# Spectrum split by parity, pixels in four quadrants of the array, the blurred part on 66 columns

## The chip, the cores and the metric

The kernel runs on one core of one Trainium2 chip. The metric is the device time of one execution in microseconds (us). Five engines matter: PE is TensorE (PEld is its weight load), ACT is ScalarE, DVE is VectorE, POOL is GpSimd, and SP is the queue from which nearly all DMAs are issued.

## The reference

The input is x, 16 images of 64 channels of 128 x 128 pixels, float32. Two layers follow each other.

```python
# layer 0: Hartley transform, 20x20 low modes mixed over channels, transformed back,
# blurred (9-tap Gauss) over all four axes, then masked along the last axis
x_ht = dht_2d(x)
out_ht[:, :, :20, :20] = compl_mul2d(x_ht[:, :, :20, :20], w1)
y = gaussian_smoothing_4d(dht_2d(out_ht) / (H * W)) * (abs(fftfreq(W)) <= 0.25)
# layer 1
h = group_norm(y)
h = irfft2(block MLP on the first 32 x 32 modes of rfft2(h)) + h     # _afno
h = h + y                                                            # residual
f = gelu(conv1x1(group_norm(h)))                                     # features
out = mean over 2 shared of gelu(conv1x1(f)) + sum over the top 4 of 16 experts of
      gate * gelu(conv1x1(f)) + h                                    # gate from the mean of f
```

`abs(fftfreq(W)) <= 0.25` holds for 65 of the 128 columns: the first 33 and the last 32.

## The kernel before

**Stages.** A *forward* stage streams x from HBM and takes the 20 x 20 Hartley modes of each image, blurred over the images, into `x2`. A *mixing* stage multiplies them with the weights (`wk`), 40 matmuls for each of 11 values of `k1`, copies the result out of PSUM into two tiles `om` (lines 298 to 303, ACT and DVE in turn), and blurs over channels. A *spectrum* stage (lines 376 to 570) takes group statistics, the 32 x 32 modes that layer 1 needs (line 548, with the 3.2 MB table `spec`) and the first half of the block MLP, and leaves per image `o1d` (MLP activations) and `od`, `ond` (the 20 x 20 modes of layer 0) in HBM. Then comes the *image* stage, which takes three quarters of the time and which most of the change is about.

**One image** in the image stage goes through these pieces:

- `spectrum`: one DMA brings `o1d[b]` into `s`, eight DMAs bring modes of layer 0 into columns 64 to 104 of the tile `bm` (the one buffer of that name, partitions x 32 x 105).
- `spectrum_f` (2 calls): 64 matmuls each for the second half of the MLP; ACT copies the PSUM tile into columns 0 to 63 of `bm` (line 629).
- `rows` (8 calls): inverse transform along the rows, for 4 channels of each half. Its matmuls (line 647) already use 64 x 64 quadrants of the array; ACT copies to `u` (line 652).
- `pixels` (8 calls): inverse transform along the columns, for 16 pixel rows. A matmul (line 669) contracts 107 rows of `u` (64 of layer 1's spectrum, 41 of layer 0's modes, 2 for the bias `b2`) with the table `inv2`, on 128 output partitions (two pixel rows x 64 channels). ACT adds a bias into `h` (line 677); DVE takes statistics of `h` (line 681).
- `norm2` (3 steps), `feature` (8 calls, lines 732 and 736), `gate` (8 steps), and 48 `group`s: a group is one expert or shared layer on a 128 x 1024 piece. PE (line 826), ACT's Gelu into `g` (line 831), and DVE's multiply-add into `h` (line 834) do one group. After the fourth expert of a piece, two DMAs store it (`store`, line 845).

**Order.** One list of pieces is sorted and emitted; each engine executes its instructions in that order. The list gives each call a place relative to the first of the image's own 48 groups:

```python
PIECES = (
    (lambda box, i: spectrum(box), (-84,)),
    (spectrum_f, (-57, -50)),
    ...
    (rows, (-50, -49, -48, -48, -48, -40, -39, -38)),
    (pixels, (-36, -32, -28, -24, -24, -24, -23, -23)),
    (group, range(NG)),
)
```

A place of -24 is thus after half of the 48 groups of the image before. ACT's part of a piece is emitted one piece later, DVE's part one further (`on_act`, `on_dve`). PSUM tiles named `pe` have three buffers of two banks, shared by all the pieces. `h` has 14 buffers of which an image uses 8; `u` and `bm` have one each. So `rows` of an image come after `pixels` of the one before it, and `spectrum` and `spectrum_f` after its `rows`.

Of the kernel before, what the change touches and what calls it, by code (L numbers as in the profile page):

```python
# [11 lines left out]
F32 = mybir.dt.float32  # L12
AF = mybir.ActivationFunctionType
ALU = mybir.AluOpType
# [4 lines left out]
NB, C, N = 16, 64, 128  # L19
K = 20  # L20
NM = K * K
CH = 100
# [7 lines left out]
HR, KC = 52, 105  # L30
KU = KC + 2
CL = C // 2
# [22 lines left out]
def constant_tables():  # L55
# [22 lines left out]
    a32 = th * np.outer(m32, n)  # L78
    inv1, inv2 = np.zeros((128, 2, N)), np.zeros((KU, N))
    for r in (0, 64):  # L80
# [5 lines left out]

    inv2[KC], inv2[KC + 1] = inv2[:32].sum(0), inv2[32:64].sum(0)
    c, s = np.cos(a32).sum(0), np.sin(a32).sum(0)
    bias = np.array([[c, s], [-s, c]])

    by_half = lambda t: t.reshape(-1, 2, 2, N // 2).transpose(0, 1, 3, 2).reshape(-1, 2 * N)
    inv1, bias = by_half(inv1), by_half(bias)

# [37 lines left out]
    for loc in range(5):  # L131
# [12 lines left out]
        "inv2": inv2,  # L144
        "bias": bias,
        "spec": chunked(spec.reshape(NM, 2 * MD * MD)),
# [13 lines left out]
def hartley_afno_moe_kernel(ctx: ExitStack, tc: tile.TileContext, a: dict, out: bass.AP):  # L160
# [26 lines left out]
    with tc.tile_pool(name="modes", bufs=1) as mp:  # L187
# [6 lines left out]
        with tc.tile_pool(name="f_x", bufs=10) as xp, tc.tile_pool(name="f_t", bufs=2) as tp, \  # L194
# [9 lines left out]
            def along_columns(b, t1):  # L204
# [20 lines left out]
                for bo in range(NB):  # L225
                    g = float(gb[bo, b])
                    if g == 0.0:
                        continue
                    to = x2[:, 0, bo, :]
                    if bo in seen:  # L230
                        nc.vector.scalar_tensor_tensor(to, xf, g, to, ALU.mult, ALU.add)
                    else:
                        nc.vector.tensor_scalar(to, xf, g, None, ALU.mult)
                        seen.add(bo)
                    if not gb[bo, b + 1:].any():
                        nc.scalar.mul(x2[0:C, 1, bo], x2[C:P, 0, bo], -1.0)
                        nc.scalar.copy(x2[C:P, 1, bo], x2[0:C, 0, bo])

# [37 lines left out]
        vec = load(const, "vec", [P, V_N])  # L276
        spec = load(sc, "spec", [CH, 4, 2 * MD * MD])
        exw = load(sc, "exw", [P, C, NE])

        with tc.tile_pool(name="m_o", bufs=1) as op, \  # L280
# [7 lines left out]
            for k1 in range(K // 2 + 1):  # L288
# [8 lines left out]
                lo, up = ps[0:C, :, :, :, 0], ps[C:P, :, :, :, 1]  # L297
                nc.scalar.copy(lok[:, k1], lo[:, :, 0])
                nc.vector.tensor_copy(upk[:, k1], up[:, :, 0])
                if k1 % (K // 2):  # L300
                    nc.scalar.copy(lok[:, K - k1, 0:1], lo[:, 0:1, 1])
                    nc.scalar.copy(lok[:, K - k1, K // 2 - 1:0:-1], lo[:, 1:, 1])
                    nc.vector.tensor_copy(upk[:, K - k1, ::-1], up[:, :, 1])


            for b0 in range(0, NB, 8):
                for cc in range(2):
# [7 lines left out]
                    for h in range(2):  # L315
# [4 lines left out]
                        else:  # L320
                            nc.vector.tensor_copy(dst, src)


    s3 = ctx.enter_context(ExitStack())
# [8 lines left out]

    b2 = kp.tile([2, C], F32, name="b2t")
    for ri in range(2):
        nc.sync.dma_start(b2[ri:ri + 1], a["b2"][32 * ri:32 * ri + 1, 0:C])
    bias = load(kp, "bias", [2, 2, N])
    b2r = kp.tile([P, 2, C], F32, name="b2r")
    b2x = dram.tile([2, N, C], F32, name="b2x")
    inv1 = load(kp, "inv1", [P, 2, N])  # L340
    inv2 = load(kp, "inv2", [KU, N])
    grp = load(kp, "grp", [P, P])
# [18 lines left out]
    nc.vector.memset(ones_e, 1.0)  # L361
    bm = kp.tile([P, CL, KC], F32, name="bm")
    nc.gpsimd.memset(bm, 0.0)
# [7 lines left out]
    with tc.tile_pool(name="s_w", bufs=2) as sw, tc.tile_pool(name="s_o", bufs=1) as so, \  # L371
# [134 lines left out]
        def prepare():  # L506
            for hf in range(2):
# [6 lines left out]
                nc.scalar.copy(v2b[C:P, hf, 1], v2[C:P, 0, cs])  # L514
            ps = pp3.tile([P, 512], F32, name="pso")
            for i in range(2):
                nc.tensor.matmul(ps[:, i * C:(i + 1) * C], lhsT=bias[:, i], rhs=b2, start=True, stop=True)
            nc.scalar.copy(b2r.rearrange("p i c -> p (i c)"), ps[:, 0:2 * C])
            nc.sync.dma_start(b2x.rearrange("i n c -> n i c"), b2r)

# [49 lines left out]
    with s3:  # L570
# [6 lines left out]
        u = up_.tile([P, N, C], F32, name="u")  # L577
        nc.sync.dma_start(u[KC:KU], b2x)

# [17 lines left out]
        def flush():  # L597
            done(0)
            while behind_d:
                behind_d.popleft()()  # L600

        def spectrum(box):

            b = box["b"]
            s = box["s"] = sp.tile([P, MD * MD], F32, name="s")
            nc.sync.dma_start(s, o1d[b].rearrange("r c k -> (r c) k"))
            for h in range(2):
                r, i = (0, 32) if h else (64, 96)
                cs = slice(h * CL, (h + 1) * CL)
                for at, q, src in ((r, 0, od), (i, 1, od), (r + 1, 21, od), (i, 21, ond)):  # L610
                    nc.sync.dma_start(bm[at:at + K, :, 64 + q:64 + q + K], src[b, :, cs, :])

        def spectrum_f(box, q):
# [13 lines left out]
            def evacuate():  # L627
                bmf = bm[:, :, 0:64].rearrange("p c (r j) -> p r c j", r=2)
                nc.scalar.copy(bmf[:, :, :, q * 16:(q + 1) * 16], ps.rearrange("p i r c -> p r c i"))
                if q:  # L630
                    box["spectrum"] = True
# [3 lines left out]
        def rows(box, q):  # L635


            if q == 0:
                if "spectrum" not in box:
                    flush()  # L640
            ps = ps2.tile([P, 2, 4, N], F32, name="pe")
            for i in range(4):
                for part, h in ((0, 0), (1, 0), (0, 1), (1, 1)):
                    k0 = C * (h ^ part)
                    rs = slice(k0, k0 + (HR if part else C))
                    cs = slice(64, KC) if part else slice(0, 64)
                    nc.tensor.matmul(ps[cs, h, i, :], lhsT=bm[rs, 4 * q + i, cs],  # L647
                                     rhs=inv1[rs, part], start=True, stop=True)

            def evacuate():  # L650
                dst = u[0:KC].rearrange("p n (h s) -> p h s n", h=2)[:, :, 4 * q:4 * q + 4, :]
                nc.scalar.copy(dst.rearrange("p h s n -> p n h s"),  # L652
                               ps[0:KC].rearrange("p h s n -> p n h s"))
                box["rows"] = q + 1

            on_act(evacuate)

        def pixels(box, t):
# [7 lines left out]
            ps = ps2.tile([P, 2, 512], F32, name="pe")  # L666
            for r in range(8):
                row = t * 8 + r
                nc.tensor.matmul(  # L669
                    ps[:, r // 4, r % 4 * N:(r % 4 + 1) * N],  # L670
                    lhsT=u[0:KU, 2 * row:2 * row + 2, :].rearrange("p h c -> p (h c)"),
                    rhs=inv2, start=True, stop=True)

# [189 lines left out]
        def step(name, make):  # L863
# [7 lines left out]

        PIECES = (
            (lambda box, i: spectrum(box), (-84,)),
            (spectrum_f, (-57, -50)),
            (feature, (-5, -4, -3, -2, -2, -2, -2, 0)),
            (step("norm", norm2), (-19, -16, -10)),
            (step("gate", gate), (2, 3, 5, 7, 8, 8, 10, 12)),
            (rows, (-50, -49, -48, -48, -48, -40, -39, -38)),
            (pixels, (-36, -32, -28, -24, -24, -24, -23, -23)),
            (group, range(NG)),  # L880
# [79 lines left out]
```

## Time and profile before

| What | us |
|---|---|
| median of 3 runs (lowest, highest) | 1857.68 (1852.98, 1859.34) |
| the profiled execution | 1848.89 |
| its span on the core | 1846.9 |
| forward stage, to the last matmul of line 212 | 0 to 253 |
| mixing, first to last matmul of line 294 | 261 to 289 |
| spectrum stage, to the first spectrum_f | 289 to 474 |
| first Gelu of a group, image 0 to image 15 | 530.1 to 1778.9 |
| end | 1846.9 |

The profile is of one execution. "Busy" is the union of an engine's instructions, and matmul ends are modelled. From the first group of one image to that of the next the trace shows 83.3 to 84.4 us (the last such step, with nothing after it to prepare, 76.5), so 15 steps make 1249 us of the 1847. The table is read with that number in mind: a saving of 1 us per image is 15 us of the whole.

### The profile page before, as it was taken

How to read it: one execution, taken by the hardware profiler on the slowest of the kernel's cores; microseconds unless marked ns; L12 is line 12 of the kernel's file. 1: busy time of each engine (PE TensorE's matmuls, PEld its weight loads, DVE VectorE, ACT ScalarE, POOL GpSimd, SP SyncE). 2: the span in 40 equal slices, each digit the busy share in tenths (PEclk: the TensorE clock that was granted, in tenths of full speed). 3: DMA queues.
4: the chain of work that ended last, by engine and by line, in shares of the span. 5: the costliest groups of instructions: out<-in, count | busy, mean ns of one | idle time of the engine just before them, and what ended most of it. 6: DMA issues, size and time to landing. Idle time of an engine off the chain costs nothing. (4 is left out here: it accounts for less than half of the span.)

```text
span 1846.9 us, 55817 instructions
## 1 busy us (share of the span) xinstructions
PE 1701.5 (92%) x24644; PEld 940.8 (51%) x24644; DVE 1270.7 (69%) x1774; ACT 1378.3 (75%) x1690; POOL 120.9 (7%) x140
## 2 busy tenths in 40 slices
PE   6777769999899999999999999999999999999996
PEld 6776765333645455454545555454545455554521
DVE  1233432322249788797979797797979797887988
ACT  2343343112488998989898999989898999989897
POOL 0000002003010101010110101010100101010110
PEclk8899988999999999999999999999999999999998
DMA  9999841115212222222332222322232322222023
GB/s 337 319 322 326 285 145 48 69 52 145 47 25 70 48 81 57 84 36 82 57 72 58 59 82 36 99 41 81 37 86 53 71 72 46 72 57 71 27 72 92
DMA packets 136129, 181.00 MB, mean 98 GB/s; under 512 B 94201, under 2 KB 95414, under 8 KB 135658
## 3 DMA queue, kind: packets, MB, share of 16 engines
q1 hardware_dynamic: 132192, 171.73, 33.1%
q0 software_dynamic: 3696, 5.71, 1.2%
q8 instruction: 193, 3.16, 0.7%
q14 instruction: 48, 0.39, 0.1%
HBM read 98.29 MB, written 79.11 MB: 96 GB/s over the span
## 5 line engine op out<-in xcount | busy, mean ns | idle before, releaser
L834 DVE SCALAR_TENSOR_TENSOR h<-g,wt,h 128x1024 f32<-128x1024 f32 x512 | 620.9, 1275 | 85.2 <-ACT g L831 85.2
L831 ACT ACTIVATE g<-pe,wl 128x1024 f32<-128x1024 f32 x512 | 539.4, 1131 | 8.9 <-PE pe L826 8.2
L826 PE MATMUL pe<-f,wl 64*64 64x512 f32 x4096 | 494.7, 600 | 1.3 <-issue 0.4
L834 DVE SCALAR_TENSOR_TENSOR h<-g,h 128x1024 f32<-128x1024 f32 x256 | 301.6, 1220 | 56.1 <-ACT g L831 56.1
L831 ACT ACTIVATE g<-pe,vec_sb 128x1024 f32<-128x1024 f32 x256 | 278.7, 1135 | 20.6 <-PE pe L826 20.4
L669 PEld LDWEIGHTS pe<-inv_sb,u 107*128 107x128 f32 x2048 | 234.4, 192 | 64.9 <-ACT g L831 33.2
L826 PEld LDWEIGHTS pe<-f,wl 64*64 64x64 f32 x4096 | 135.6, 132 | 237.3 <-ACT g L831 98.6
L826 PE MATMUL pe<-f,shw 64*64 64x512 f32 x2048 | 252.9, 604 | 0.0
L669 PE MATMUL pe<-inv_sb,u 107*128 107x128 f32 x2048 | 248.8, 279 | 3.2 <-ACT g L831 1.9
L677 ACT ACTIVATE h<-pe,gs 128x1024 f32<-128x1024 f32 x128 | 142.6, 1115 | 73.2 <-PE pe L669 57.3
L250 PE MATMUL ps<-fwd_sb,xt 128*64 128x64 f32 x4096 | 141.5, 232 | 51.0 <-issue 43.1
L681 DVE BATCH_NORM_STATS2 stats<-h 128x6 f32<-128x512 f32 x256 | 160.1, 679 | 25.9 <-ACT h L677 25.8
L250 PEld LDWEIGHTS ps<-fwd_sb,xt 128*64 128x64 f32 x4096 | 135.9, 147 | 54.7 <-issue 46.6
L647 PE MATMUL pe<-inv_sb,bm 64*64 64x128 f32 (+1 forms) x4096 | 144.8, 275 | 1.2 <-issue 1.2
L736 ACT ACTIVATE f<-pe,fb 128x1024 f32<-128x1024 f32 x128 | 144.3, 1137 | 2.2 <-PE pe L732 2.2
L647 PEld LDWEIGHTS pe<-inv_sb,bm 64*64 64x64 f32 (+1 forms) x4096 | 118.5, 124 | 48.1 <-ACT f L736 24.3
L253 ACT COPY t<-ps 128x320 f32<-128x320 f32 x128 | 54.0, 427 | 114.4 <-PE ps L250 114.0
L732 PE MATMUL pe<-h,fs 64*64 64x512 f32 x1024 | 133.9, 611 | 1.6 <-DVE n L709 1.6
L652 ACT COPY u<-pe 105x1024 f32<-105x1024 f32 x128 | 127.4, 1043 | 3.9 <-PE pe L647 2.9
L219 DVE TENSOR_TENSOR xm<-ps,pn 64x20 f32<-64x20 f32 x32 | 5.5, 171 | 172.5 <-ACT pn L215 172.2
L548 PE MATMUL psx<-spec_sb,ot 100*64 100x512 f32 x512 | 115.6, 594 | 0.0
L806 POOL DMA_INDIRECT wl<-exd,ati x64 | 66.9, 1045 | 697.4 <-ACT g L831 605.4
(164 smaller groups left out, 1163.5 us busy)
## 6 DMA issues: line engine op xcount, KB each, us to landing
xt<-in_x_dram SPq DMA_DIRECT2D x128, 512.0 KB
out_dram<-h SPq DMA_DIRECT2D x256, 256.0 KB
o1d<-o SPq DMA_DIRECT2D x16, 512.0 KB
s<-o1d SPq DMA_DIRECT2D x16, 512.0 KB
bm<-od SPq DMA_DIRECT2D x96, 50.0 KB
wk<-in_w_dram SPq DMA_DIRECT2D x11, 320.0 KB
wn<-in_w_dram SPq DMA_DIRECT2D x11, 320.0 KB
spec_sb<-in_spec_dram SPq DMA_DIRECT2D x1, 3200.0 KB
```

Of the source, the lines that this page charges most:

```text
L250: nc.tensor.matmul(ps[cols, i, :], lhsT=xt[:, i, cols], rhs=fwd1, start=True, stop=True)
L548: nc.tensor.matmul(ps[ri * C:(ri + 1) * C], lhsT=ot[:, kc, b * C:(b + 1) * C], rhs=spec[:, kc, ri * 1024 + n * 512:ri * 1024 + (n + 1) * 512],
L647: nc.tensor.matmul(ps[cs, h, i, :], lhsT=bm[rs, 4 * q + i, cs], rhs=inv1[rs, part], start=True, stop=True)
L652: nc.scalar.copy(dst.rearrange("p h s n -> p n h s"), ps[0:KC].rearrange("p h s n -> p n h s"))
L669: nc.tensor.matmul(ps[:, r // 4, r % 4 * N:(r % 4 + 1) * N], lhsT=u[0:KU, 2 * row:2 * row + 2, :].rearrange("p h c -> p (h c)"), rhs=inv2, ...
L677: nc.scalar.activation(h, ps, AF.Identity, bias=gs1[:, 1, box["b"]:box["b"] + 1])
L681: nc.vector.bn_stats(box["stats"][:, 2 * t + p, :], h[:, p])
L732: nc.tensor.matmul(ps[p * C:(p + 1) * C, half], lhsT=box["fs"][rows_], rhs=box["h"][t][rows_, p], start=True, stop=True)
L736: nc.scalar.activation(f, ps, AF.Gelu, bias=box["fb"], accum_out=box["sums"][:, t:t + 1])
L826: nc.tensor.matmul(ps[half * C:(half + 1) * C, p], lhsT=w[rows_], rhs=f[rows_, half], start=True, stop=True)
L831: nc.scalar.activation(g, ps, AF.Gelu, bias=bias)
L834: nc.vector.scalar_tensor_tensor(h, g, share(), h, ALU.mult, ALU.add)
```

## The change

Four things change together.

1. `bm` gets 128 columns (layer 0's modes in columns 64 to 127, padded with zeros). `rows` makes twice as many matmuls, each with half as many moving columns: the even and the odd pixel rows of the output go to the lower and the upper 64 partitions of PSUM and of `u`, and layer 1's and layer 0's parts lie side by side along `u`'s free axis. The lines and loops are otherwise the same.
2. `pixels` makes, for 4 row pairs, 4 matmuls of 128 moving columns (layer 1's part) and 4 of 66 (layer 0's part, the first and last 33 columns only), all on 64 x 64 quadrants, adding in PSUM.
3. The bias `b2` no longer comes as two extra rows of `u`: it is added when `spectrum_f`'s PSUM tile is copied to `bm`, which DVE now does in two additions of 128 x 512 in place of ACT's one copy of 128 x 1024. The tiles `b2r`, `b2x`, `bias` with their matmuls and DMAs go.
4. Places change: `spectrum` is divided (the load of `s` at -86, the eight loads of `bm` at -76), and `spectrum_f`, `rows`, `pixels`, `feature`, `norm2`, `gate` are put elsewhere. In the stages before, mixing's copies go to ACT for even and to DVE for odd `k1`, the second of two finishing copies of `x2` goes from ACT to DVE, and the tables `spec` and `exw` are loaded in the program after the mixing instead of before it. In SP's queue nothing stands between the two places: the loads are still issued after the table `w1` and before `v2`.

```diff
-HR, KC = 52, 105
-KU = KC + 2
+HR, KC = 52, 105
+MH = 33
...
                         nc.scalar.mul(x2[0:C, 1, bo], x2[C:P, 0, bo], -1.0)
-                        nc.scalar.copy(x2[C:P, 1, bo], x2[0:C, 0, bo])
+                        nc.vector.tensor_copy(x2[C:P, 1, bo], x2[0:C, 0, bo])
...
-                nc.scalar.copy(lok[:, k1], lo[:, :, 0])
-                nc.vector.tensor_copy(upk[:, k1], up[:, :, 0])
+                copy = nc.vector.tensor_copy if k1 % 2 else nc.scalar.copy
+                copy(lok[:, k1], lo[:, :, 0])
+                copy(upk[:, k1], up[:, :, 0])
                 if k1 % (K // 2):
-                    nc.scalar.copy(lok[:, K - k1, 0:1], lo[:, 0:1, 1])
-                    nc.scalar.copy(lok[:, K - k1, K // 2 - 1:0:-1], lo[:, 1:, 1])
-                    nc.vector.tensor_copy(upk[:, K - k1, ::-1], up[:, :, 1])
+                    copy(lok[:, K - k1, 0:1], lo[:, 0:1, 1])
+                    copy(lok[:, K - k1, K // 2 - 1:0:-1], lo[:, 1:, 1])
+                    copy(upk[:, K - k1, ::-1], up[:, :, 1])
...
+    sc2 = on_modes.enter_context(tc.tile_pool(name="s_c2", bufs=1, side="right"))
+    spec = load(sc2, "spec", [CH, 4, 2 * MD * MD])
+    exw = load(sc2, "exw", [P, C, NE])
...
-    bm = kp.tile([P, CL, KC], F32, name="bm")
+    bm = kp.tile([P, CL, 2 * C], F32, name="bm")
...
             def evacuate():        # of spectrum_f
                 bmf = bm[:, :, 0:64].rearrange("p c (r j) -> p r c j", r=2)
-                nc.scalar.copy(bmf[:, :, :, q * 16:(q + 1) * 16], ps.rearrange("p i r c -> p r c i"))
+                for i in (0, 8):
+                    j = q * 16 + i
+                    nc.vector.tensor_tensor(bmf[:, :, :, j:j + 8],
+                                            ps[:, i:i + 8].rearrange("p i r c -> p r c i"),
+                                            b2.unsqueeze(3).to_broadcast([P, 2, CL, 8]), ALU.add)
...
-            ps = ps2.tile([P, 2, 4, N], F32, name="pe")           # rows
+            ps = ps2.tile([P, 2, 4, 2, C], F32, name="pe")
             for i in range(4):
-                for part, h in ((0, 0), (1, 0), (0, 1), (1, 1)):
-                    k0 = C * (h ^ part)
-                    rs = slice(k0, k0 + (HR if part else C))
-                    cs = slice(64, KC) if part else slice(0, 64)
-                    nc.tensor.matmul(ps[cs, h, i, :], lhsT=bm[rs, 4 * q + i, cs],
-                                     rhs=inv1[rs, part], start=True, stop=True)
+                for part in range(2):
+                    for h, p in ((0, 0), (1, 1), (1, 0), (0, 1)):
+                        rs = slice(h * C, h * C + (HR if part else C))
+                        nc.tensor.matmul(ps[p * C:(p + 1) * C, h, i, part, :],
+                                         lhsT=bm[rs, 4 * q + i, part * C:(part + 1) * C],
+                                         rhs=inv1[rs, part, p * C:(p + 1) * C], start=True, stop=True)
...
-            for r in range(8):                                    # pixels
-                row = t * 8 + r
-                nc.tensor.matmul(
-                    ps[:, r // 4, r % 4 * N:(r % 4 + 1) * N],
-                    lhsT=u[0:KU, 2 * row:2 * row + 2, :].rearrange("p h c -> p (h c)"),
-                    rhs=inv2, start=True, stop=True)
+            quadrants = ((0, 0), (1, 1), (0, 1), (1, 0))
+            for r in range(4):
+                n = 2 * (4 * t + r)
+                for p, half in quadrants:
+                    k = slice(p * C, (p + 1) * C)
+                    nc.tensor.matmul(ps[half * C:(half + 1) * C, p, r * N:(r + 1) * N],
+                                     lhsT=u[k, n + half, :], rhs=inv2[k, 0:N], start=True, stop=False)
+                for p, half in quadrants:
+                    k = slice(p * C, (p + 1) * C)
+                    to = ps[half * C:(half + 1) * C, p, r * N:(r + 1) * N]
+                    nc.tensor.matmul(bass.AP(to.tensor, to.offset, [to.ap[0], (N - MH, 2), (1, MH)]),
+                                     lhsT=u[k, C + n + half, :],
+                                     rhs=inv2[k, N:].rearrange("k (a n) -> k a n", a=2),
+                                     start=False, stop=True)
...
-            (lambda box, i: spectrum(box), (-84,)),
-            (spectrum_f, (-57, -50)),
-            (feature, (-5, -4, -3, -2, -2, -2, -2, 0)),
-            (step("norm", norm2), (-19, -16, -10)),
-            (step("gate", gate), (2, 3, 5, 7, 8, 8, 10, 12)),
-            (rows, (-50, -49, -48, -48, -48, -40, -39, -38)),
-            (pixels, (-36, -32, -28, -24, -24, -24, -23, -23)),
+            (lambda box, i: spectrum_in(box), (-86,)),
+            (lambda box, i: spectrum(box), (-76,)),
+            (spectrum_f, (-76, -49)),
+            (feature, (-6, -4, -3, -2, -2, -2, -2, -1)),
+            (step("norm", norm2), (-20, -17, -12)),
+            (step("gate", gate), (2, 5, 6, 8, 9, 10, 12, 14)),
+            (rows, (-48, -48, -48, -37, -33, -32, -32, -29)),
+            (pixels, (-27, -26, -25, -24, -24, -24, -24, -24)),
             (group, range(NG)),
```

## The prediction

> **What bounds the kernel now.** The image stage is 15 steps of 83.8 us, so I start from the page's busy times and its costliest groups, then cut one step in two.
>
> ```profile
> PE 1701.5 (92%) x24644; PEld 940.8 (51%) x24644; DVE 1270.7 (69%) x1774; ACT 1378.3 (75%) x1690; POOL 120.9 (7%) x140
> L669 PE MATMUL pe<-inv_sb,u 107*128 107x128 f32 x2048 | 248.8, 279 | 3.2 <-ACT g L831 1.9
> L677 ACT ACTIVATE h<-pe,gs 128x1024 f32<-128x1024 f32 x128 | 142.6, 1115 | 73.2 <-PE pe L669 57.3
> L629 ACT COPY bm<-pe 128x1024 f32<-128x1024 f32 x32 | 33.8, 1056 | 12.3 <-PE pe L622 12.0
> ```
>
> PE looks full, but its ends are modelled. The third line says more: ACT, doing `pixels`, stood idle 57.3 us for PE's line 669. The busy times by stretch divide the step of image 6 (1047.75 to 1131.57) into the time from the first `pixels` to the end of the last, and the rest (columns: stretch, length, then busy us and count of PE, PEld, DVE, ACT, POOL, clock, DMA share, GB/s):
>
> ```profile
> 1047.75:1076.04 28.29, 28.04 (x244) 18.60 (x244) 27.18 (x33) 23.44 (x23) 3.97 (x4) 1.00 0.32 55
> 1076.04:1131.57 55.53, 53.43 (x870) 23.70 (x862) 43.17 (x57) 53.78 (x66) 1.44 (x2) 1.00 0.25 69
> ```
>
> In the first stretch (8 `pixels`, 14 groups) PE sets the time: ACT idles 4.9 of 28.3 us. In the rest ACT does: 53.8 of 55.5 busy. PE's timeline gives the price of a step, by differences of starts:
>
> ```profile
> 1064.79 5.62 PE L669 MATMUL pe<-inv_sb,u 107*128 107x128 f32 x48
> 1070.35 1.09 PE L826 MATMUL pe<-f,wl 64*64 64x512 f32 x8
> 1071.37 3.84 PE L669 MATMUL pe<-inv_sb,u 107*128 107x128 f32 x32
> 1075.13 3.66 PE L826 MATMUL pe<-f,wl 64*64 64x512 f32 x32
> ```
>
> Three `pixels` take 5.56 us, two 3.76: 1.80 each, plus 0.16 for the change of array form. ACT's timeline in that stretch shows the price of PE being late:
>
> ```profile
> 1066.88 1.11 ACT L677 ACTIVATE h<-pe,gs 128x1024 f32<-128x1024 f32 x1 [0.40 <-PE pe L669]
> 1068.67 1.11 ACT L677 ACTIVATE h<-pe,gs 128x1024 f32<-128x1024 f32 x1 [0.67 <-PE pe L669]
> 1070.45 1.11 ACT L677 ACTIVATE h<-pe,gs 128x1024 f32<-128x1024 f32 x1 [0.67 <-PE pe L669]
> ```
>
> They come 1.79 us apart, PE's pace; elsewhere ACT starts one every 1.01 us (the same timeline has four Gelus of line 831 from 1062.36 in 4.13 us, the last lasting 1.11).
>
> **What the Trainium skill says.** "TensorEngine Tiling (Array Packing)", § Key Properties: different tiles load and multiply in parallel, and changing the tiling mode drains the array. The trace agrees: a `rows` step puts 32 matmuls of 128 columns on four quadrants in 0.87 us, 109 ns for four, while line 669 needs 112 ns (1.80/16) for one on the full array; the 0.16 us would be the drain. The same page, § PSUM Bottleneck: tiling speeds TensorE, not the copying out of PSUM; ACT, the next bound, is not relieved by quadrants. "TensorE: Matmul & The Clock Gate", § Back-to-back issue gap, gives small matmuls a floor of about 25 ns; this trace shows one per 14 ns in `spectrum_f` (below), so the trace is used. The same page, § LDWEIGHTS, prices a load at columns/1.2: 53 ns for 64 columns. The trace's loads last 134 ns for 64, 114 for 41, 110 for 32, about the same slope (0.75 ns a column), but overlap.
>
> **The change, part by part.** Every float32 matmul of the program is two instructions (4096 of line 826 for 512 groups of four).
>
> *pixels.* Removed: 16 instructions on the full array. Added: 32 of 128 columns and 32 of 66, in quadrants. A wave of four takes 109 ns at 128 columns; a group's wave of 512 takes about 0.43 us (8 instructions, 0.86 us), so time goes with columns and 66 take 56 ns. 8 x 0.109 + 8 x 0.056 = 1.32 us, against 1.80 or 1.96. This density, a new weight load and a matmul every 14 ns, is shown by `spectrum_f`:
>
> ```profile
> 1005.15 0.22 PE L622 MATMUL pe<-v2a,s 128*32 128x64 f32 x1
> 1005.16 0.22 PE L622 MATMUL pe<-v2b,s 128*32 128x64 f32 x1
> 1005.17 0.22 PE L622 MATMUL pe<-v2a,s 128*32 128x64 f32 x1
> 1005.17 0.22 PE L622 MATMUL pe<-v2b,s 128*32 128x64 f32 x1
> 1005.21 0.22 PE L622 MATMUL pe<-v2a,s 128*32 128x64 f32 x1
> ```
>
> Four in about 55 ns, but with loads of 32 columns; 64-column loads every 14 ns are not shown. Line 312 comes nearest: four quadrants, 64 moving columns, loads of 64 and 36; 192 matmuls span 5.35 us at the half clock, 28 ns, which is 14 at full clock. Bounds: 1.32 us if loads stay hidden, 1.71 (64 x 26.7 ns) if 64 columns cost twice a load of 32. I take 1.33.
>
> *rows.* 64 instructions of 64 columns for 32 of 128: 16 x 56 ns = 0.90 us for 0.87. Bounds 0.88 and 1.71, as above; I take 0.95. PE gets 10,236 more matmuls and as many loads in all; the instruction queue moved 3.16 MB for 2 x 24,644, 64 bytes each, so 1.3 MB more, 0.1 MB an image. In the one timeline row of 31 matmuls of line 647 (1106.67, 1.37 us for 1.10) PE loses 0.27 us after a dense run; I allow 0.7 us an image for more of these, 0 to 1.5.
>
> *bm's copy.* ACT loses 2 x 1.02 us an image. DVE gains 4 additions of 512 elements from PSUM. Nearest rows: 0.75 (line 552, contiguous) and 1.22 us (line 483, an addition's like with scattered writes); so 3.0 to 4.9 us, taken 3.4. Cover: DVE is busy 70.4 of 83.8 us, its longest idle time being the features at the step's end, where the second copy falls. If that cover goes, DVE's total of 74, with the 3.4 us a step that it waits for POOL, sets the pace at 77. While DVE is behind, the PSUM buffer is held and PE has two left; and a `spectrum_f` of 1.92 us no longer gives ACT work, so ACT may run dry for up to 1 us each.
>
> *New places.* `bm`'s eight loads now stand at place 20 of the 48, right ahead of the first stores (groups 22, 23), in SP's queue. They take 5 us to issue (1046.14 to 1051.1), and wait for `rows` of place 19. `pixels` 6 and 7 at place 24 need the two `h` buffers that these stores free; today ACT waits 8.0 us in all for `out_dram<-h`. PE needs about 12 us from place 20 to there (1.9 + 5 x 1.33 + 4 x 0.9), the stores come at about the same time: 0 to 3 us an image, taken 0.6. `s` and `bm` themselves come 28 places, some 45 us, before `rows`: hidden.
>
> *Before the images.* The copies of `x2`: ACT did ten of 0.53 us in a row from 256.0 to 261.4 and PE waited 8.17 for it; with five on DVE beside ACT, -1.8 us. Mixing: 28 us for 11 k1, copies strictly in turn at 2.05 us each; now two k1 are copied at once at 1.9 us each, and PE (40 x 27 ns or, at half clock, 53) comes into the cycle: (1.9 + 0.3 + 1.1 to 2.1)/2 = 1.6 to 2.1 us per k1. Saves 0 to 9 us since PE's waits for its own issue (3.25 and 1.33 us) stay; taken 5. Bias matmuls: -0.6. `spec` and `exw`: nothing, because SP's queue has them where they were: issued at 261, read by line 548 from 321 on; if they did wait for the mixing, they would be issued at 289, and 3.7 MB at the 285 GB/s of that slice take 13 us, still before 321. The first image has its 8 `pixels` alone: 8 x (1.79 - 1.33) = -3.7.
>
> **The sum for one step.** First stretch: PE 8 x 1.33 + 14 x 0.9 = 23.2, ACT 22 x 1.03 = 22.7, which now balance; with 0.6 for the stores and 0.5 because five `pixels` come in a row, 24.3 for 28.3: -4.0. The rest: ACT 53.8 - 2.0 = 51.8; PE 53.4 + 0.6 + 0.7 by busy time, not lower than before; so of ACT's 2.0 I count a quarter: 55.0 for 55.5. A step is then 79.3. 15 x 4.5 = 67.5, and 3.7 + 5 + 1.8 + 0.6 = 11.1 before: **-78.6 us**. The last 68 us (DVE's 1.2 us per group) stay. The profiled execution of 1848.9 goes to 1770; it lay 8.8 below the median of 1857.7, so the median goes to **about 1780**.
>
> **Rivals.**
> (A) *The gain turns into waits of three equal engines* (0.18). With ACT 74, DVE 77 with its waits, PE 73 to 75, nothing is left to absorb late buffers; a step ends at 81.8: 15 x 2.0 + 11 = 41 off, 1817. For it: DVE's row of 85.2 us of idle time ahead of line 834 shrinks with no other cover. Against it: `g` has 7 buffers to let DVE lag.
> (B) *Weight loads bind: slower* (0.09). If a 64-column load costs PE 26.7 ns, `rows` are 1.71 (+6.5 us an image), `pixels` 1.71 (-0.9 to -2). PE is over ACT in both stretches: 27 + 59 = 86; 15 x 2.2 less 7 before = +26, 1884. It decides from about 22 ns per load, where the two cancel. For it: nothing in the trace loads 64 columns every 14 ns. Against: line 312.
> (C) *No net change* (0.03): `h` buffers late by some 5 us an image eat it, 1857.
> The main case has 0.70, 1755 to 1803.
>
> **How the numbers follow.** A measurement of this kernel can tell about 0.3% (5.6 us) from no change. Faster: main case and A, 0.88; same 0.03; slower 0.09. The range goes from 1748 (a step of 77.5, the DVE floor, and the full 11) to 1830, which holds the main case and most of A, and leaves out B and C.
>
> **What would show it.** Right: `pixels` at about 1.33 us in a row and no 0.67 us waits of line 677; `rows` 0.9 to 1.0; the step at 79; line 294's span near 23 us. Wrong: `rows` near 1.7 (B); waits of line 677's successor for `out_dram<-h`, or PE's loads released by DVE's new addition (A, C).

## The result, and the profile after

The changed kernel takes **1931.14 us** (median of 4 runs, 1922.86 to 1935.15) against 1857.66: a ratio of **1.039 [1.035, 1.044]**, 4% slower, where 1780 was forecast. Its profiled execution has a span of 1932.0 us, 85.1 more than before.

By stage, from the trace: the mixing takes 29.4 us from its first to its last matmul (27.5 before); from there to the first group's Gelu it is 252.3 us (241.1 before); from one image's first group to the next one's 88.7 us (83.75 before; these are means without the first and the last step, and all 15 steps together take 71 us more); the tail after the last image's first group is unchanged at 68 us.

First the busy times and the groups of the page, with one line of the groups by line (columns: busy us and mean ns, then idle time ahead of the group on its engine and what ended it):

```profile
PE 1690.2 (87%) x34880; PEld 920.8 (48%) x34880; DVE 1322.8 (68%) x1859; ACT 1340.1 (69%) x1638; POOL 152.1 (8%) x140
L649 PE MATMUL pe<-inv_sb,bm 52*64 52x64 f32 (+1 forms) x8192 | 157.5, 226 | 50.2 <-issue 37.7
L649 PEld LDWEIGHTS pe<-inv_sb,bm 52*64 52x64 f32 (+1 forms) x8192 | 151.4, 139 | 99.0 <-issue 52.6
L680 PE MATMUL pe<-inv_sb,u 64*64 64x66 f32 x4096 | 173.2, 219 | 18.4 <-issue 18.3
L688 ACT ACTIVATE h<-pe,gs 128x1024 f32<-128x1024 f32 x128 | 142.8, 1115 | 71.6 <-PE pe L680 67.5
L629 DVE TENSOR_TENSOR bm<-pe,b2t 128x512 f32<-128x512 f32 x64 | 41.1, 683 | 39.3 <-PE pe L620 39.3
```

Every engine that was thought to bind is less busy, or little more, than before: PE 11 us less, ACT 38 less, DVE 52 more but at 68%. The new entries are idle times of PE that end with "issue": no semaphore and no DMA that the profile knows released them. Line 647 had 1.2 us of it, its successor 649 has 37.7.

The forecast's price of a `pixels` was right where nothing disturbs it. PE's timeline inside a `pixels` of line 675 (128 columns) and 680 (66 columns):

```profile
1119.17 0.43 PE L675 MATMUL pe<-inv_sb,u 64*64 64x128 f32 x8
1119.39 0.33 PE L680 MATMUL pe<-inv_sb,u 64*64 64x66 f32 x8
1119.50 0.43 PE L675 MATMUL pe<-inv_sb,u 64*64 64x128 f32 x8
1119.72 0.33 PE L680 MATMUL pe<-inv_sb,u 64*64 64x66 f32 x8
```

A pair of waves starts every 0.33 us, four pairs are 1.33 us. ACT follows at that pace and then falls out of it, as its timeline a little later shows:

```profile
1119.10 1.12 ACT L688 ACTIVATE h<-pe,gs 128x1024 f32<-128x1024 f32 x1
1120.44 1.11 ACT L688 ACTIVATE h<-pe,gs 128x1024 f32<-128x1024 f32 x1 [0.22 <-PE pe L680]
1121.78 1.11 ACT L688 ACTIVATE h<-pe,gs 128x1024 f32<-128x1024 f32 x1 [0.23 <-PE pe L680]
1124.73 1.12 ACT L688 ACTIVATE h<-pe,gs 128x1024 f32<-128x1024 f32 x1 [1.83 <-PE pe L680]
```

1.34, 1.34, then 2.95 us. PE's timeline has the reason, here and in the third of three `rows`:

```profile
1073.34 0.52 PE L649 MATMUL pe<-inv_sb,bm 64*64 64x64 f32 x23
1076.61 0.38 PE L649 MATMUL pe<-inv_sb,bm 52*64 52x64 f32 x4 [2.75 <-issue]
...
1122.74 0.28 PE L680 MATMUL pe<-inv_sb,u 64*64 64x66 f32 x3
1124.35 0.28 PE L680 MATMUL pe<-inv_sb,u 64*64 64x66 f32 x3 [1.33 <-issue]
```

In the middle of a loop of equal matmuls, with all operands there, PE stands still for 2.75 and 1.33 us. The next view is what PE itself waited for from 600 to 1700 us, some 12 images (columns: waited us in total, times, longest):

```profile
PE pe L649 <- issue: 30.2, 15, 3.5
PE pe L680 <- issue: 13.0, 10, 2.2
PE pe L675 <- issue: 11.5, 11, 1.9
...
PE pe L837 <- DVE bm L629: 4.5, 8, 1.0
```

**Where the stalls lie.** I numbered all instructions of PE in order, loads and semaphore instructions included, and measured from the start of one to the start of the next. Over 1.1 us and ahead of an instruction that waits for no semaphore there are 54 such stalls (124 us in all), and all 54 come after instruction number 193 + a multiple of 256, counted from 1. Before the change there are 25 (58 us), all but one in the forward stage and the mixing, which both kernels have. Each of the 54 ends 1.2 to 1.7 us after a packet of 16,384 bytes has landed on queue 8. The lists of DMA queues of the kernel before, of the changed one, and of the first experiment below that halves instructions (packets, MB, share):

```profile
q8 instruction: 193, 3.16, 0.7%
```

```profile
q8 instruction: 274, 4.49, 1.0%
```

```profile
q8 instruction: 209, 3.42, 0.8%
```

274 packets of 256 instructions of 64 bytes are 70,144 instructions; the trace has 70,117 on PE. So this queue is PE's program, brought in blocks of 256. And in all three traces two packets never start less than **3.32 us** apart (3.26 in all the traces of this case): 77 instructions per us at most, or 79. A packet itself takes 1.0 us, and its share of the DMA engines is 1%, so this is not a lack of bandwidth: each block comes late. The packets show how late. In every trace there is one packet for each end of a block that PE passes; it starts at most 5.0 us before PE passes that end, and the packet after it never starts before that point, so never more than one block lies ready in advance. In 30 of the changed kernel's 31 stalls from the first `spectrum_f` on, the next packet starts 1.0 to 1.6 us after PE has gone on. These 1.0 us, the packet's 1.0 and the 1.2 before PE can use it add up to the 3.3. A block that is needed sooner finds PE waiting.

Now the demand, counted with the loads: `spectrum_f` is 256 instructions in 1.92 us, 133 per us, before and after. `rows` were 64 in 0.87 us, 74 per us, just under the supply; they are 128 in 0.93, **138 per us**. `pixels` were 32 in 1.80 us, 18 per us; they are 128 in 1.34, **95 per us**. A group is 16 in 0.9 us, 18 per us. The block that is there in advance hides a short excess. Right after a `spectrum_f` at place -49 the new list puts three `rows` into one place, and five `pixels` into another. There the stalls are.

Behind a stall in `rows` the granted clock is at half for 3.4 or 6.8 us: from the first group's Gelu on, `rows` have nine stalls of 2.6 to 3.8 us, eight are followed by such a stretch, and there is no other but at the very end (2.7 us an image). "TensorE: Matmul & The Clock Gate", § What's actually happening (Part 1), has the clock fall to half after about 3.4 us with PE idle, for windows of that length. The trace agrees on the length of the windows (3.413 us or twice that); the pauses ahead of them, with a few slow matmuls among them, are partly shorter.

### The profile page after: what moved, and what is told of

Same layout as the page of the kernel before. It is cut to its first block, busy times and chain, and to the rows that moved or that the text cites. A ratio compares the mean times of both kernels' runs of the same rounds, so it can differ in the third digit from the quotient of the medians.

```text
span 1932.0 us, 76365 instructions
## 1 busy us (share of the span) xinstructions
PE 1690.2 (87%) x34880; PEld 920.8 (48%) x34880; DVE 1322.8 (68%) x1859; ACT 1340.1 (69%) x1638; POOL 152.1 (8%) x140
## 5 line engine op out<-in xcount | busy, mean ns | idle before, releaser
L842 ACT ACTIVATE g<-pe,wl 128x1024 f32<-128x1024 f32 x512 | 548.5, 1151 | 47.5 <-PE pe L837 46.1
L837 PE MATMUL pe<-f,wl 64*64 64x512 f32 x4096 | 509.5, 600 | 16.8 <-DMA wl<-exd,ati 7.6
L837 PE MATMUL pe<-f,shw 64*64 64x512 f32 x2048 | 268.0, 627 | 0.5 <-issue 0.5
L649 PE MATMUL pe<-inv_sb,bm 52*64 52x64 f32 (+1 forms) x8192 | 157.5, 226 | 50.2 <-issue 37.7
L675 PE MATMUL pe<-inv_sb,u 64*64 64x128 f32 x4096 | 186.2, 270 | 14.2 <-issue 13.8
L649 PEld LDWEIGHTS pe<-inv_sb,bm 52*64 52x64 f32 (+1 forms) x8192 | 151.4, 139 | 99.0 <-issue 52.6
L680 PE MATMUL pe<-inv_sb,u 64*64 64x66 f32 x4096 | 173.2, 219 | 18.4 <-issue 18.3
L655 ACT COPY u<-pe 128x1024 f32<-128x1024 f32 x128 | 127.7, 1021 | 69.4 <-PE pe L649 69.2
L680 PEld LDWEIGHTS pe<-inv_sb,u 64*64 64x64 f32 x4096 | 156.1, 133 | 20.1 <-issue 20.0
L675 PEld LDWEIGHTS pe<-inv_sb,u 64*64 64x64 f32 x4096 | 139.8, 134 | 47.9 <-issue 41.7
L817 POOL DMA_INDIRECT wl<-exd,ati x64 | 96.9, 1514 | 766.0 <-ACT g L842 654.2
```

Of the source, the lines that this page charges most:

```text
L649: nc.tensor.matmul(ps[p * C:(p + 1) * C, h, i, part, :], lhsT=bm[rs, 4 * q + i, part * C:(part + 1) * C], rhs=inv1[rs, part, p * C:(p + 1) ...
L655: nc.scalar.copy(dst.rearrange("p h s n -> p n h s"), ps.rearrange("p h s a n -> p (a n) h s"))
L675: nc.tensor.matmul(ps[half * C:(half + 1) * C, p, r * N:(r + 1) * N], lhsT=u[k, n + half, :], rhs=inv2[k, 0:N], start=True, stop=False)
L680: nc.tensor.matmul(bass.AP(to.tensor, to.offset, [to.ap[0], (N - MH, 2), (1, MH)]), lhsT=u[k, C + n + half, :], rhs=inv2[k, N:].rearrange( ...
L837: nc.tensor.matmul(ps[half * C:(half + 1) * C, p], lhsT=w[rows_], rhs=f[rows_, half], start=True, stop=True)
L842: nc.scalar.activation(g, ps, AF.Gelu, bias=bias)
```

## Experiments

Three theories were put against each other. **S**: the supply of instructions, as above. **D**: `bm`'s additions on DVE come late, and PE waits for them or for their PSUM buffer. **P**: the new places of `rows` and `pixels` do harm by themselves (late `h` buffers, a late `u`). Each ratio below is to the kernel before on the same chip (medians 1852.8 to 1854.3).

**1. The changed arithmetic at the places of before** (all pieces are put back; two lines are shown).

```diff
...
-            (rows, (-48, -48, -48, -37, -33, -32, -32, -29)),
-            (pixels, (-27, -26, -25, -24, -24, -24, -24, -24)),
...
+            (rows, (-50, -49, -48, -48, -48, -40, -39, -38)),
+            (pixels, (-36, -32, -28, -24, -24, -24, -23, -23)),
...
```

> The changed kernel's matmuls and copies, put back at the places of the kernel before (pixels one per four groups, rows at -50 to -38, spectrum_f at -57 and -50). Theory S (instruction supply: PE reads its program in blocks of 256 instructions, and stands still without any semaphore where a block is used up faster than the next one comes, in the places where spectrum_f, rows or pixels stand close together): the pixels' stalls go, those of rows after spectrum_f stay; 3 to 4 us of stalls per image instead of 7.3, 1850 to 1885 us. Theory D (DVE's addition for bm starves ACT and holds up rows and PSUM): it is still on DVE, so 1910 or more. Theory P (the new places as such, by buffers and stores): back to the forecast step of 79 to 80, about 1790.

Measured: 2000.94 us, 1.080 [1.076, 1.084], 93.8 us a step. S's forecast failed, P's by far the most, and only D's holds. PE's waits and ACT's from 600 to 1700 us:

```profile
PE pe L837 <- DVE bm L629: 56.8, 12, 5.2
PE pe L837 <- ACT h L688: 47.9, 25, 3.4
```

```profile
ACT h L688 <- DMA out_dram<-h: 30.1, 18, 3.2
```

At the old places the hand-over of `bm` meets DVE when it lags furthest: once per image a group's matmul waits 4.7 us on average for the PSUM buffer that line 629 still reads. So D is real at these places, and late `h` buffers are too; the change's own list avoids both (4.5 us in all for `bm`, above). P as it was put, harm by the new places, does not explain the loss: at the old ones the same arithmetic is slower still. PE's stalls by "issue" fall from 57.4 us to 13.9 in the same stretch, but there is more half clock, 8.4 us a step against 2.7.

**2. The arithmetic of before at the new places**, the load of `s` divided from `spectrum` as the list requires.

```diff
...
-            (rows, (-50, -49, -48, -48, -48, -40, -39, -38)),
-            (pixels, (-36, -32, -28, -24, -24, -24, -23, -23)),
...
+            (rows, (-48, -48, -48, -37, -33, -32, -32, -29)),
+            (pixels, (-27, -26, -25, -24, -24, -24, -24, -24)),
...
```

> The kernel before with the new places alone (the load of s ahead of spectrum as in the change). Theory S: 2200 instructions per image on PE as before, stalls under 1.5 us per image, so 1845 to 1875 us. Theory P: the loss of the changed kernel shows here already, 1900 or more. Theory D: as before, about 1858.

Measured: 1876.54, 1.0115 [1.008, 1.015], 84.9 us a step; PE's stalls by "issue" are 1.3 us in all from 600 to 1700. With the old arithmetic the places cost 22 us (the change costs 73): at 1.8 us each, five `pixels` in a row keep ACT waiting for PE (77.0 us from 600 to 1700, against 44.5 for line 677 before).

**3. Before, with each matmul of `rows` as two of 64 columns**: the same columns and results, twice the instructions.

```diff
-                    nc.tensor.matmul(ps[cs, h, i, :], lhsT=bm[rs, 4 * q + i, cs],
-                                     rhs=inv1[rs, part], start=True, stop=True)
+                    for n0 in (0, C):
+                        nc.tensor.matmul(ps[cs, h, i, n0:n0 + C], lhsT=bm[rs, 4 * q + i, cs],
+                                         rhs=inv1[rs, part, n0:n0 + C], start=True, stop=True)
```

> The kernel before, where each matmul of rows (128 moving columns) is made as two of 64: same data, same sums, same columns through the array, twice the instructions (32 more matmuls and loads per rows). Theory S: stalls without semaphores of 1.5 to 3 us per image appear in rows, 1880 to 1905 us. Theories D and P: nothing of theirs is touched; rows cost 0.93 instead of 0.87 us, so within 10 us of 1858.

Measured: 1873.47, 1.009 [1.006, 1.012]: 19 us, less than S expected and more than its rivals. A step grows by 0.7 us only; that the slower pieces between the `rows` let the queue catch up is the likely reason. But from the mixing's end to the first Gelu it is 252.1 us, 11.0 more than before and just what the changed kernel takes (252.3): there the first image's eight `rows` come in a row, with nothing slow between them. PE's timeline in these `rows`, before (first line, all in one) and in this run:

```profile
481.62 6.30 PE L647 MATMUL pe<-inv_sb,bm 52*41 52x128 f32 x210
```

```profile
485.63 2.17 PE L648 MATMUL pe<-inv_sb,bm 52*41 52x64 f32 x128 [0.86 <-issue]
489.36 2.17 PE L648 MATMUL pe<-inv_sb,bm 52*41 52x64 f32 x128 [1.56 <-issue]
493.10 2.17 PE L648 MATMUL pe<-inv_sb,bm 52*41 52x64 f32 x128 [1.56 <-issue]
```

128 matmuls with their loads are 256 instructions. They run through in about 2 us, then PE stands still until 3.73 us have passed since the block before began: 69 instructions per us. The kernel before makes these `rows` without a pause.

**4. The changed kernel with `rows` and `pixels` spread**

```diff
-            (lambda box, i: spectrum(box), (-76,)),
-            (spectrum_f, (-76, -49)),
+            (lambda box, i: spectrum(box), (-81,)),
+            (spectrum_f, (-66, -57)),
...
-            (rows, (-48, -48, -48, -37, -33, -32, -32, -29)),
-            (pixels, (-27, -26, -25, -24, -24, -24, -24, -24)),
+            (rows, (-48, -46, -44, -42, -40, -38, -36, -34)),
+            (pixels, (-32, -30, -29, -28, -27, -26, -24, -23)),
```

> The changed kernel with its dense pieces set apart, so that two groups of 16 instructions stand between rows and at least one between pixels: rows at -48, -46, ... -34, pixels at -32, -30, -29, -28, -27, -26, -24, -23, spectrum_f at -66 and -57, bm's loads at -81. Theory S: a block of 256 instructions lasts 4 us or more nearly everywhere, stalls under 1.5 us per image, a step of 79 to 81 us, 1785 to 1815 us. Theory D: DVE's additions are still there, 1910 or more. Theory P: it would depend on buffers; no fall is foreseen by it.

Measured: 1979.83, 1.067 [1.064, 1.071]. The forecast of S failed, because the new places brought in what experiment 1 has (and 9.3 us of half clock a step), though the stalls by "issue" fall to 13.9 us. ACT's and PE's waits from 600 to 1700 us:

```profile
ACT h L688 <- DMA out_dram<-h: 55.8, 24, 4.7
```

```profile
PE pe L837 <- DVE bm L629: 29.5, 12, 2.8
```

Earlier `pixels` want `h` buffers whose store has not left, and `spectrum_f` is again handed over while DVE lags. Here moving work cured one cause by paying for another; S had to be tested without moving anything.

**5. The changed kernel with half the instructions, same columns, same places.**

```diff
-                        nc.tensor.matmul(ps[p * C:(p + 1) * C, h, i, part, :],
-                                         lhsT=bm[rs, 4 * q + i, part * C:(part + 1) * C],
-                                         rhs=inv1[rs, part, p * C:(p + 1) * C], start=True, stop=True)
+                    nc.tensor.matmul(ps[p * C:(p + 1) * C, h, i].rearrange("p a n -> p (a n)"),
+                                     lhsT=bm[rs, 4 * q + i, 0:C], rhs=inv1[rs, 0], start=True, stop=True)
...
-                    nc.tensor.matmul(ps[half * C:(half + 1) * C, p, r * N:(r + 1) * N],
-                                     lhsT=u[k, n + half, :], rhs=inv2[k, 0:N], start=True, stop=False)
...
+                    nc.tensor.matmul(ps[half * C:(half + 1) * C, p, o:o + N + 2 * MH],
+                                     lhsT=u[k, n + half, :], rhs=inv2[k], start=True, stop=True)
```

> The changed kernel with half the instructions in rows and pixels and the same streamed columns: a quadrant's rows matmul is one of 128 columns (it was two of 64), a quadrant's pixel matmul one of 194 columns (it was 128 and 66). Left out: the second of the two products that the pairs add up, so the output is not the reference's. DVE's additions to bm, the places of all steps, ACT's and the stores' work are as in the changed kernel. S (the supply of instructions: 512 fewer instructions a step with their loads, no longer more than the queue delivers): the stalls of PE without a semaphore at block ends fall from 6 to 7 us a step to under 1.5, the half-clock stretches in the steady state go, the period falls from 88.7 to 79-83 us and the time to 1780-1835 us. D (the additions on DVE): the period stays at 86 or more, 1890 us or more. P (the places of rows and pixels): also 1890 us or more, since nothing is moved.

Measured: **1833.89 us, 0.991 [0.988, 0.994]**, 82.9 us a step, 238.3 us from the mixing's end to the first Gelu, no half clock from step to step. That is 97 us below the changed kernel (some 90 when each is set against the kernel before on its own chip: 1.039 and 0.991), with PE's streams as long (0.87 us for `rows`, 1.31 for `pixels`) and DVE's additions, ACT's work, the stores and all places as they were: S carries the loss. Weight loads are halved with the matmuls, so this run alone does not part the two; but where nothing stalls, `rows` with all their loads take 0.93 us for 0.87, and the stalls lie at ends of blocks. `rows` here no longer read the columns of `bm` that DMAs fill; no wait for these shows in the changed kernel. PE's stalls by "issue" fall from 57.4 us to 0.4. From 600 to 1700 us, ACT's waits in the changed kernel, then in this one:

```profile
ACT g L842 <- PE pe L837: 52.9, 69, 3.4
ACT h L688 <- PE pe L680: 48.5, 74, 2.7
ACT u L655 <- PE pe L649: 47.2, 23, 4.3
```

```profile
ACT g L833 <- PE pe L828: 51.8, 68, 1.6
ACT h L679 <- PE pe L673: 12.9, 61, 0.7
ACT h L679 <- DMA out_dram<-h: 11.8, 15, 1.8
ACT u L653 <- PE pe L648: 8.2, 14, 0.6
```

Waits for `rows` fall from 47.2 to 8.2 us, those for `pixels` from 48.5 to 12.9. The wait of `g` stays; part of it has another cause (below). The run also gives a measure of what the arithmetic could bring: with the supply out of the way it is 1% faster than before, not 4%.

**6. The changed kernel with `bm` copied by ACT**

```diff
-                for i in (0, 8):
-                    j = q * 16 + i
-                    nc.vector.tensor_tensor(bmf[:, :, :, j:j + 8],
-                                            ps[:, i:i + 8].rearrange("p i r c -> p r c i"),
-                                            b2.unsqueeze(3).to_broadcast([P, 2, CL, 8]), ALU.add)
+                nc.scalar.copy(bmf[:, :, :, q * 16:(q + 1) * 16], ps.rearrange("p i r c -> p r c i"))
```

> The changed kernel with bm taken from PSUM by one ACT copy per call, as before the change, in place of DVE's two additions; left out is the addition of b2. S: the stalls of PE at block ends stay (5 us a step or more) and the time stays within 1% of 1931 us: the wait of rows for DVE (1 us a step) goes, and ACT gets 2 us a step more. D (DVE's hand-over in the wrong place is what costs): the period falls to 82 us or less, 1830 us or less.

Measured: 1917.16, 1.036 [1.032, 1.039]. PE's stalls stay (54.2 us by "issue" at lines 645, 671 and 676, where the changed kernel has 54.7 at 649, 675 and 680), so S stands. D is worth 14 us at most at the new places: with each ratio taken on its own chip it is 7 us, and the intervals of the two ratios overlap. Here are this kernel's waits of PE from 600 to 1700 us:

```profile
PE pe L645 <- issue: 30.8, 37, 2.8
PE pe L671 <- issue: 12.8, 12, 1.9
PE pe L676 <- issue: 10.6, 10, 1.7
```

**7. Half the instructions in `pixels` alone, and 8. in `rows` alone**: the two halves of experiment 5's diff. Of 7:

```diff
-                    nc.tensor.matmul(ps[half * C:(half + 1) * C, p, r * N:(r + 1) * N],
-                                     lhsT=u[k, n + half, :], rhs=inv2[k, 0:N], start=True, stop=False)
...
+                    nc.tensor.matmul(ps[half * C:(half + 1) * C, p, o:o + N + 2 * MH],
+                                     lhsT=u[k, n + half, :], rhs=inv2[k], start=True, stop=True)
```

and of 8:

```diff
-                        nc.tensor.matmul(ps[p * C:(p + 1) * C, h, i, part, :],
...
+                    nc.tensor.matmul(ps[p * C:(p + 1) * C, h, i].rearrange("p a n -> p (a n)"),
```

> As the kernel with half the instructions, in pixels alone: 256 instructions a step fewer. Left out: the second of a quadrant's two products in pixels, so the output is not the reference's. S in blocks of 256: the stalls inside the pixels go (2.3 us a step in the changed kernel, with the half-clock stretches after them) and so do those of the eight pixels ahead of the first group; those of three rows in one place stay (2 us a step). Period 84-86.5 us, time 1845-1885 us: between the changed kernel and the one with both halved.

> As the kernel with half the instructions, in rows alone: 256 instructions a step fewer. Left out: the second product of rows, so the output is not the reference's. S in blocks of 256: the stalls of three rows in one place go (2 us a step), those in the five pixels of place -24 stay (2.3 us a step), as do those of the eight pixels ahead of the first group. Period 85-87 us, time 1860-1895 us.

Measured: `pixels` alone 1925.76, 1.037 [1.032, 1.042], 89.0 us a step; `rows` alone 1862.75, 1.005 [1.003, 1.007], 84.3 us a step. I had expected about equal parts; 7 missed its range, 8 met it. ACT's waits of 7 (first) and of 8, from 600 to 1700 us, show how unequal they are:

```profile
ACT u L655 <- PE pe L649: 77.5, 47, 5.1
ACT h L681 <- PE pe L675: 11.3, 49, 1.0
```

```profile
ACT h L686 <- PE pe L678: 46.0, 79, 3.0
ACT u L653 <- PE pe L648: 7.7, 14, 0.6
```

Each halving removes its own waits, but in 7 those for `rows` grow from 47.2 to 77.5 us, and the sum (88.8 for 95.7) is nearly as before. PE's own stalls in `rows` grow too, from 30.2 us to 45.3 (line 649, by "issue"). With `rows` at 74 instructions per us again, 68 us come back; the 95 per us of `pixels` then cost 29 (1862.8 against 1833.9). The two are not a sum: 5 and 68 alone, 97 together.

**9. `spectrum_f` in four calls of half the size, `rows` one per place; 10. and 11. only the bunched places opened.** All three keep the whole arithmetic.

9, where each call of `spectrum_f` makes 8 of the 16 values of `i` and one addition (the loads of `bm` also move, to -80, and `norm2` to -18, -15 and -11):

```diff
-            (spectrum_f, (-76, -49)),
+            (spectrum_f, (-79, -77, -49, -48)),
...
-            (rows, (-48, -48, -48, -37, -33, -32, -32, -29)),
-            (pixels, (-27, -26, -25, -24, -24, -24, -24, -24)),
+            (rows, (-47, -45, -43, -41, -39, -37, -35, -33)),
+            (pixels, (-29, -28, -27, -26, -25, -24, -22, -21)),
```

10, and 11 below it, have these lines in place of the same two:

```diff
+            (rows, (-47, -46, -45, -37, -34, -33, -32, -29)),
+            (pixels, (-27, -26, -25, -24, -24, -23, -22, -22)),
```

```diff
+            (rows, (-47, -45, -43, -37, -34, -32, -31, -29)),
+            (pixels, (-28, -27, -26, -25, -24, -24, -23, -22)),
```

> The changed arithmetic with the demand for instructions spread in time: spectrum_f in four calls of half the size (one DVE addition each) two in each of its two stretches, rows one per place instead of three together, pixels from -29 to -21, loads and norm moved with them. S: the steps that had three rows or five pixels in one place no longer outrun the queue; PE's stalls at block ends fall to under 3 us a step, and as no hand-over by DVE is put into the stretch in which DVE is late (as it was in the kernel with rows spread from -48 to -34), the period is 80-84 us and the time 1790-1850 us. D and P: waits for bm's addition or for h buffers whose store has not left come in instead, 87 us a step or more, 1900 us or more.

> The changed kernel with its full arithmetic, only the bunched places opened by one or two: rows at -47, -46, -45, -37, -34, -33, -32, -29, pixels at -27, -26, -25, -24, -24, -23, -22, -22, so that a group's 16 or so slow instructions stand between two dense runs of 128. S: stalls at block ends fall from 4.8 us a step (those over 0.7 us) to under 2, nothing else comes in, period 83-86 us, time 1830-1880 us. P (places): new waits for h buffers or u eat it up, 1900 us or more.

> As the kernel before it in this call, opened further: rows at -47, -45, -43, -37, -34, -32, -31, -29, pixels at -28, -27, -26, -25, -24, -24, -23, -22. S: stalls at block ends under 1.5 us a step, period 82.5-85.5 us, time 1825-1870 us. P: an early row meets DVE's late addition to bm, or a late pixel a store that has not left: 1890 us or more.

Measured: 1895.74 (1.024 [1.021, 1.027]), 1895.60 (1.022 [1.019, 1.025]) and 1901.09 (1.024 [1.020, 1.029]); 86.2 to 86.5 us a step. 30 to 36 us come back, about a third of the 97 and less than expected in all three. Stalls by "issue" go from 57.4 us to 8.2, 28.6 and 28.4 from 600 to 1700, and new waits of PE come in, of 9 and of 10 (with the stalls that 10 keeps in `rows`):

```profile
PE pe L620 <- DVE bm L628: 23.8, 26, 1.1
PE pa L706 <- DVE mv L694: 14.9, 12, 1.7
```

```profile
PE pe L649 <- issue: 16.5, 13, 2.5
PE pa L707 <- DVE mv L695: 16.3, 12, 1.7
```

`pixels` that end two or three places later seem to leave `norm2` too little time, as PE waits for the statistics; quarters of `spectrum_f` so close together wait for DVE's addition for the one before. No version with the whole arithmetic beats the kernel before.

## Why the prediction was wrong, point by point

**The step that failed** is a single term: "I allow 0.7 us an image for more of these, 0 to 1.5". It took the 10,236 added matmuls and loads for a cost per dense run, and the 1.3 MB of program for a transfer of no weight. Measured, PE's stalls by "issue" from 600 to 1700 us grow from 0.4 to 57.4 us, 4.6 an image, besides 2.7 us an image at half clock. In time it is the 97 us between the changed kernel and experiment 5, where the term had 15 x 0.7 = 10.5: by the two profiles 81 us in the 15 steps and 14 from the mixing's end to the first Gelu. The sign follows from it: of the 151 us between 1780 and 1931 this term holds most of the 97. The forecast did give "slower" a chance of 0.09, but by weight loads that bind, and that is not what happened. The page of before had the parts: 193 packets, 24,644 matmuls, and a forward stage where PE stood still for "issue". What was not taken from the trace is the spacing of those packets.

**The other 54 us** (1833.9 against 1780) are sums that were too good:

- *The step.* Without the stalls it is 82.9, not 79.3. ACT's work fell as worked out (75.15 busy in the step below, 77.40 in the same cut of before), but its idle time, which was to fall, rose by 1.0 us in these two cuts. That is near rival A, which had 81.8. The sum had cut the step as the old places do, 8 `pixels` among 14 groups; the change's own list leaves 3 groups between its first and last `pixels`. In these cuts ACT's idle time from the first `pixels` to the last falls only from 4.3 to 3.2 us, and in the rest of the step it rises from 2.4 to 4.4. Busy times by stretch of one step of before (first line) and of experiment 5, cut from one image's first `h` to the next one's:

```profile
1049.84:1133.84 84.00, 81.65 (x1110) 42.30 (x1114) 70.37 (x90) 77.40 (x88) 5.56 (x7) 1.00 0.28 65
```

```profile
1055.55:1138.28 82.73, 77.86 (x1234) 37.41 (x1234) 72.86 (x95) 75.15 (x85) 7.71 (x6) 1.00 0.22 61
```

PE, ACT and DVE stand at 78, 75 and 73 of 82.7: no engine is full, and each waits for the others. Two of the waits were named in the forecast, at too low a price or none. ACT runs dry at a `spectrum_f` that no longer brings it work (1.50 us at 1054.24 in experiment 5's timeline, where "up to 1 us" was allowed), and PE then waits for the PSUM buffer that DVE's additions hold (600 to 1700 us):

```profile
PE pe L828 <- DVE bm L629: 16.6, 13, 1.5
```

That is 1.3 us an image in experiment 5.
- *Mixing*: taken -5, measured +1.9 in the changed kernel. Over the ten profiles with the changed copies the span is 25.7 to 30.0 us, with the old ones 27.5 to 28.0: no gain that these runs show. PE's stalls "for its own issue", which I left in the sum as they were, lie at the same ends of blocks (2.0 and 4.8 us in the changed kernel).
- *x2*: taken -1.8, the wait is 6.79 us for 8.17: -1.4. *The first image's `pixels`*: taken -3.7; experiment 5 gains 2.8 from the mixing's end to the first Gelu, so most of it is there once the supply is.

**What was right.** `pixels` at 1.33 us (1.34), `rows` at 0.95 (0.93), so rival B is out: 64-column loads do come every 14 ns (0.93/64) and stay hidden. DVE's additions were taken at 3.4 us an image in all; they are busy 41.1 us over 16 images, so 2.6. The waits of ACT for `out_dram<-h` stay small at the new places (1.8 us in all; 11.8 in experiment 5 from 600 to 1700, 0.9 an image where 0.6 was taken); rival C did not happen. The 0.67 us waits inside a row of `pixels` became 0.22, as said.

**What stays open.** Why no more than one block is held in advance, and whether that can be changed, no run here shows. Why the halving of `pixels` alone gave nothing back is shown only as a shift of stalls and waits to `rows`. And no run with the whole arithmetic and without the stalls exists, so the 1% of experiment 5 stands for a kernel that leaves out half the products.

## What to carry to other kernels

Count instructions per us of each dense stretch, loads included, and set them beside the closest spacing of the instruction queue's packets in the same trace; here pieces that stayed above that rate until the block in advance was used up stalled at the ends of blocks, whatever their columns and quadrants promised. A split into more, smaller matmuls was therefore not free at equal streaming time, and it cost most where dense pieces followed each other. When such a stall is suspected, halve the instructions at equal columns rather than move the pieces: moving brought in waits of its own.

## What the runs showed of the hardware that I had not expected

- PE's instructions come in packets of 16,384 bytes (256 instructions), never less than 3.32 us apart in three traces (3.32, 3.36 and 3.34 us), so at most 77 per us; PE goes on 1.2 to 1.7 us after the packet has landed. Never more than one block lies ready in advance, so PE runs faster than that only until it is used up (experiment 3: 256 instructions per 3.73 us in a long dense run).
- `rows` with 64 or 128 moving columns, so with twice the loads for the same columns, differ by 0.06 us in 0.9 (0.87 and 0.93) as long as instructions are there: four quadrants hide a 64-column load of 133 ns every 14 ns.
- A DVE addition of 128 x 512 from PSUM that writes runs of 8 takes 683 ns, little more than half of the 1.22 us of line 483's with scattered writes.
